# Where a block of expert results is parked between PSUM and memory: a buffer group of its own, eight deep

## The chip, the core and the metric

The kernel runs on one core of one Trainium2 chip. The metric is the device time of one execution in microseconds (us), and the figure given for a kernel is the median of its runs. The core has a matrix engine (PE, with its weight loads, PEld, beside it), a vector engine (DVE), a scalar engine (ACT), a general engine (POOL) and SyncE (SP), which here issues most DMAs. Each engine runs its own list of instructions in order, and one engine waits for another, or for a DMA to land, on a semaphore.

## The reference, cut to what matters

Thirty-two sequences of 56 tokens, each of width 256, with a context of 1500 rows each, go through two layers of a cross-attention and a feed-forward block of experts:

```python
x = x + _L0_xattn_ref(_layernorm(x), ctx_2048, ...)     # a decayed sum over the context, projected
x = x + _L0_ffn_ref(_layernorm(x), gate_w, w_gate, w_up, w_down)   # 16 experts of 176, 6 per token
x = x + _L1_xattn_ref(_layernorm(x), ctx_2048, mask)    # softmax attention over the context
x = x + _L1_ffn_ref(_layernorm(x), ...)                 # 2 experts of 1024, 1 per token
```

The change stands in the second of these. For each expert e the reference computes

```python
g = h @ w_gate[e].T
u = h @ w_up[e].T
out = jax.nn.silu(g) * u @ w_down[e].T
y = y + cw[:, e:e + 1] * out          # cw is zero outside a token's six experts
```

## The kernel before, in words

The program has four stages, one after the other: the context sums with the routing of tokens to experts (to about 210 us of the profile), the first experts (to about 513 us), the attention (to about 602 us) and the second experts (to the end).

In the first-experts stage the tokens have been sorted by expert into 99 blocks of 128 rows (`NB0`), padded where an expert's rows do not fill a block. `expert_blocks` (L769) runs over the blocks with a software pipeline written out by hand: in step t it issues the gate and up product of block t (`gate_up`, L778), turns the product of block t-1 (`turn`, L799), turns the input rows of block t+1 (`turned_rows`, L192), and issues the down product of block t-2 (`down`, L807). A step has twelve matmuls: four for `gu` (L785), two transposes of `hs` (L803), two transposes of the gathered rows (L195), and four for `y` (L812).

The order on every engine of this stage is the order of the Python code (`manual_schedule`, L928); no planner moves anything. Waits follow from the tile pools: a tile of a pool with n buffers waits until the tile n before it under the same tag has been used for the last time. The pools of the stage are `wk` (three buffers a tag: `sg`, `hs`, `hT`, `xT`, `yb`), `rt` (single tiles), `xbp` (eight buffers, used for the gathered rows `xb`), `resp` (six, for results `g` fetched back), and four PSUM pools of two banks each.

When a block's down product is finished, `done` (L949) copies it from PSUM to a tile `yb` on ACT (L951) and issues on SP a store of 128 KB to its place in `ys0` in device memory (L952). So `yb` of block n is written when the store of block n-3 has landed. On ACT the order of one step is: `sg` of block t (L791), `xT` of block t+1 (L197), `yb` of block t-2 (L951).

On SP each step has the store and, beside it, a part of other transfers that `side` (L1036) issues: windows of the context, 384 KB each (L174), in steps 1 to 16; the residual rows, 2 MB, in step 17 (L1050); a row of the mask (L1055) in steps 18 to 49, each with a register load of its start; and zeros, 771 KB each (L1067), five times between steps 18 and 30. On POOL each step has the gather of a block seven ahead (`rows_of`, L941), and in most steps a gather `result` (L853) of finished results from `ys0` for an early token group, which DVE adds to the residual (L1029).

After the stage the attention begins: SP loads sixteen further context windows into new buffers (`extra`, L174), and POOL gathers the remaining results from `ys0` with an adding DMA (`added`, L1317), which needs every store landed.

Of the kernel before, what the change touches and what calls it, by code (L numbers as in the profile page):

```python
# [8 lines left out]
F32 = mybir.dt.float32  # L9
# [10 lines left out]
P = 128  # L20
B, S, D, T = 32, 56, 256, 1500
# [37 lines left out]
def xattn_ffn_kernel(  # L59
# [174 lines left out]
    with tc.tile_pool(name="p1", bufs=1) as p1, tc.tile_pool(name="p3", bufs=3) as p3, tc.tile_pool(  # L234
        name="xn", bufs=4
    ) as xnp, tc.tile_pool(name="z", bufs=4) as zp, tc.tile_pool(name="p1_ps", bufs=5, space=PSUM) as ps, tc.tile_pool(
        name="p1_acc", bufs=2, space=PSUM
# [529 lines left out]
        V.tensor_copy(ei, ep[0:1, 0:P])  # L767

    def expert_blocks(nb, nq, f, w, ei, wk, ptr, pgu, pht, py, rows_of, done, ahead, wgt=None, side=None, xT0=None):  # L769

        fp = f // nq
# [35 lines left out]
        def down(i, u):  # L807
            if u == 0:
                y[i] = py.tile([P, 512], F32, tag="y", name="y")
            a = hT.pop((i, u))  # L810
            for c in range(2):
                PE.matmul(  # L812
                    y[i][:, 0:D], lhsT=a[:, c * P : (c + 1) * P],
                    rhs=w[0:h, bass.ds(at[i] + (u * piece + doff + c * D), D)],
                    start=(u == 0 and c == 0), stop=(u == nq - 1 and c == 1),
                )
            if u == nq - 1:
                done(i, y.pop(i))
# [109 lines left out]
    with tc.manual_schedule(  # L928
        engines={ET.PE, ET.DVE, ET.Activation, ET.SP, ET.Pool}
    ), tc.tile_pool(name="f0", bufs=3) as wk, tc.tile_pool(name="f0r", bufs=1) as rt, tc.tile_pool(  # L930
        name="f0x", bufs=8
    ) as xbp, tc.tile_pool(name="res0", bufs=6) as resp, tc.tile_pool(
        name="f0_tr", bufs=2, space=PSUM
    ) as ptr, tc.tile_pool(name="f0_gu", bufs=2, space=PSUM) as pgu, tc.tile_pool(
        name="f0_ht", bufs=2, space=PSUM
# [11 lines left out]
            return xb  # L947

        def done(i, y):  # L949
            yb = wk.tile([P, D], F32, tag="yb", name="yb")  # L950
            A.copy(yb, y[:, 0:D])  # L951
            nc.sync.dma_start(out=ys0[i * P : (i + 1) * P, :], in_=yb)  # L952

# [82 lines left out]
        def side(t):  # L1036
# [50 lines left out]
        expert_blocks(  # L1087
            NB0, 1, F0, w0_sb.rearrange("p e w -> p (e w)"), ei,
            wk, ptr, pgu, pht, py, rows_of, done, 7, wgt, side,
        )  # L1090
        assert not ways_ and not todo and not sums and not steps[NR]
# [20 lines left out]
    with tc.manual_schedule(  # L1112
        engines={ET.PE, ET.DVE, ET.Activation, ET.SP, ET.Pool}
    ), tc.tile_pool(name="at", bufs=2) as at, tc.tile_pool(name="ex", bufs=1) as ex, tc.tile_pool(name="at_x", bufs=4, space=PSUM) as px, tc.tile_pool(
        name="at_sc", bufs=1, space=PSUM
    ) as psc, tc.tile_pool(name="at_pt", bufs=2, space=PSUM) as ppt, tc.tile_pool(
        name="at_o", bufs=1, space=PSUM
# [271 lines left out]
    with tc.tile_pool(name="f1", bufs=3) as wk, tc.tile_pool(  # L1389
        name="f1_tr", bufs=2, space=PSUM  # L1390
    ) as ptr, tc.tile_pool(name="f1_gu", bufs=2, space=PSUM) as pgu, tc.tile_pool(
        name="f1_ht", bufs=2, space=PSUM
# [41 lines left out]
    with tc.If(nc.values_load(bad[0:1, 0:1], min_val=0, max_val=1)), tc.tile_pool(  # L1434
        name="g", bufs=2
    ) as gp, tc.tile_pool(name="g1", bufs=1) as g1, tc.tile_pool(
        name="g_tr", bufs=2, space=PSUM
    ) as ptr, tc.tile_pool(name="g_gu", bufs=2, space=PSUM) as pgu, tc.tile_pool(
        name="g_y", bufs=1, space=PSUM
# [175 lines left out]
```

## Time and profile before

| | |
|---|---|
| median of 3 runs | 755.1 us (752.46 to 756.65) |
| profiled execution, its own time | 789.92 us |
| span of its profile | 788.0 us |
| PE busy in the span | 680.0 us (86%) |
| ACT busy / DVE busy / POOL busy | 242.2 / 404.6 / 354.0 us |
| copies `yb` (L951) | 99, 375 ns each, 37.1 us |
| mean granted PE clock | 0.945 |

The profile is of one execution, and that one took 34.8 us longer than the median of the others. Busy shares are of the engine, not of its list of waits: an engine that waits on a semaphore is idle. Where an instruction waits for more than one semaphore, the compiler puts a separate wait (EVENT_SEMAPHORE) ahead of it, which the engine's own list runs in order too. Ends of matmuls are modelled in the profile. For waits, the profile names the instruction that came last by its own clock; where none fits it says "remote" or "unknown queue".

### The profile page before, as it was taken

The page shows a single profiled execution, that of the slowest core. Times are in us where ns is not written, and L with a number is a line of the kernel's source. Part 1 is how long each engine was busy: PE and PEld are TensorE (multiplying, and loading weights), DVE is VectorE, ACT ScalarE, POOL GpSimd, SP SyncE. Part 2 cuts the span into 40 slices and gives each one's busy share as a digit, 9 for nine tenths or more (in the row PEclk, how much of TensorE's full clock was granted, in tenths as well). Part 3 has the DMA queues.
Part 4 walks back from the last instruction along what each step waited for, and adds up shares of the span by engine and source line. Part 5 has one row for each costly group of instructions (what it writes and reads, how often), then busy time and mean ns, then how long its engine had stood idle before and what let it go on. Part 6 is the DMA issues. An engine that isn't in the chain of part 4 may idle for free.

```text
span 788.0 us, 13691 instructions
## 1 busy us (share of the span) xinstructions
PE 680.0 (86%) x4147; PEld 447.8 (57%) x4147; DVE 404.6 (51%) x1386; ACT 242.2 (31%) x716; POOL 354.0 (45%) x444
## 2 busy tenths in 40 slices
PE   3477988887789889889899889899797999999995
PEld 3334545554467667556667566666464566666663
DVE  3568677788436436234444345667587333233321
ACT  0123233333134333333333333366463111111110
POOL 5355566643343465556656665457542411122110
PEclk9879799997699999899999999999899999999998
DMA  8969899999258976334434444387961200110100
GB/s 260 351 258 376 321 346 381 359 340 238 72 161 269 329 224 197 107 106 137 133 114 131 133 133 134 107 251 181 257 224 48 94 13 21 41 35 27 33 27 18
DMA packets 71426, 137.69 MB, mean 175 GB/s; under 512 B 7859, under 2 KB 43844, under 8 KB 71348
## 3 DMA queue, kind: packets, MB, share of 16 engines
q1 hardware_dynamic: 56612, 100.84, 37.4%
q0 software_dynamic: 14736, 35.90, 16.9%
q8 instruction: 39, 0.64, 0.3%
q14 instruction: 39, 0.32, 0.1%
HBM read 110.07 MB, written 27.29 MB: 174 GB/s over the span
## 4 chain that ended last, share of the span: by engine, by line
PE 72%; DVE 7%; DMA 5%; ACT 3%; issue 3%; POOL 3%; another core or an unknown queue 1%; POOLq 0%; ACTq 0%; DVEq 0%
PE gu L785 29%; PE y L812 18%; PE acc L325 6%; PE tp L803 4%; PE tp L195 4%; DMA xr<-ys,back 4%; ACT xT L197 2%; PE owned L593 1%; POOL xr L1318 1%; PE bp L467 1%; PE lp L505 1%; POOL xn L491 1%; PE sT L459 1%; PE tp L913 1%
## 5 line engine op out<-in xcount | busy, mean ns | idle before, releaser
L785 PE MATMUL gu<-w_sb,xT 128*128 x396 | 142.1, 482 | 23.9 <-ACT xT L197 19.7
L943 POOL DMA_INDIRECT xb<-xn,idx x99 | 96.6, 976 | 103.1 <-PE tp L195 52.1
L791 ACT ACTIVATE sg<-gu 128x176 f32<-128x176 f32 (+1 forms) x159 | 54.4, 342 | 239.5 <-PE gu L785 206.9
L797 DVE SCALAR_TENSOR_TENSOR hs<-sg,wgt,gu 128x176 f32<-128x176 f32 x99 | 39.3, 397 | 158.4 <-ACT sg L791 136.3
L785 PE MATMUL gu<-ring,xT 128*128 x240 | 112.9, 593 | 0.5 <-issue 0.5
L785 PEld LDWEIGHTS gu<-w_sb,xT 128*128 128x128 f32 x396 | 73.6, 194 | 61.9 <-ACT xT L197 27.5
L812 PE MATMUL y<-w_sb,hT 88*128 x396 | 103.6, 384 | 0.8 <-ACT yb L951 0.8
L856 POOL DMA_INDIRECT g<-ys,early x78 | 74.0, 949 | 33.5 <-issue 18.0
L795 DVE TENSOR_TENSOR hs<-sg,gu 128x256 f32<-128x256 f32 x60 | 25.2, 421 | 112.5 <-ACT sg L791 110.2
L803 PEld LDWEIGHTS tp<-ident,hs 128*88 128x88 f32 (+1 forms) x318 | 41.3, 131 | 61.4 <-issue 48.4
L812 PEld LDWEIGHTS y<-w_sb,hT 88*128 88x128 f32 x396 | 68.6, 193 | 7.1 <-ACT yb L951 1.0
L1423 POOL DMA_INDIRECT out<-ob,ti x15 | 14.9, 990 | 127.4 <-DVE ob L1420 127.1
L805 DVE COPY hT<-tp 88x256 f32<-88x256 f32 (+1 forms) x159 | 66.0, 415 | 3.8 <-PE y L812 2.8
L197 ACT COPY xT<-tp 128x256 f32<-128x256 f32 x130 | 48.4, 372 | 56.9 <-PE tp L195 39.3
L785 PEld LDWEIGHTS gu<-ring,xT 128*128 128x128 f32 x240 | 45.3, 190 | 33.0 <-issue 30.1
L803 PE MATMUL tp<-ident,hs 128*88 128x128 f32 (+1 forms) x318 | 61.6, 276 | 0.7 <-DVE mv L871 0.6
L812 PE MATMUL y<-ring,hT 128*128 x240 | 61.7, 380 | 0.0
L951 ACT COPY yb<-y 128x256 f32<-128x256 f32 x99 | 37.1, 375 | 61.2 <-PE y L812 31.0
L325 PE MATMUL acc<-ring,cz 128*32 128x256 f32 x768 | 54.9, 444 | 0.3 <-DVE cz L301 0.3
L195 PE MATMUL tp<-ident,xb 128*128 128x128 f32 x228 | 44.8, 279 | 2.4 <-issue 2.4
L432 POOL TENSOR_SCALAR z<-xr,mva,rsa 128x256 f32<-128x256 f32 x16 | 23.0, 1437 | 49.6 <-DVE xr L479 45.4
L812 PEld LDWEIGHTS y<-ring,hT 128*128 128x128 f32 x240 | 41.0, 190 | 3.3
(306 smaller groups left out, 1000.8 us busy)
## 6 DMA issues: line engine op xcount, KB each, us to landing
ring<-in_cx SPq DMA_DIRECT2D x32, 1536.0 KB
ys<-yb SPq DMA_DIRECT2D x99, 128.0 KB
ring<-in_cx SPq DMA_DIRECT2D x16, 384.0 KB
extra<-in_cx SPq DMA_DIRECT2D x16, 384.0 KB
xs<-zrow SPq DMA_DIRECT2D x5, 771.0 KB
w_sb<-in_wg SPq DMA_DIRECT2D x2, 1408.0 KB
w_sb<-in_wu SPq DMA_DIRECT2D x2, 1408.0 KB
xn<-xn SPq DMA_DIRECT2D x16, 128.0 KB
```

The costliest lines, as they stand in the source:

```text
L195: PE.transpose(tp[:, k * P : (k + 1) * P], xn[:, k * P : (k + 1) * P], ident)
L197: A.copy(xT.rearrange("p k c -> p (k c)"), tp[:, 0 : KD * P])
L325: PE.matmul(acc[Q * g : Q * g + Q, 0:D], lhsT=cz[:, j, 1 - h : 1 - h + Q], rhs=c[:, j, :], start=(h == 0 and m == 0), stop=(h == 1 and m = ...
L785: PE.matmul(gu[:, 0 : 2 * fp], lhsT=xT[i][:, k, :], rhs=w[:, bass.ds(at[i] + (u * piece + k * 2 * fp), 2 * fp)], start=(k == 0), stop=(k = ...
L791: A.activation(sg, gu[:, 0:fp], AF.Silu)
L797: V.scalar_tensor_tensor(hs[i, u], sg, wgt[:, i : i + 1], up, ALU.mult, ALU.mult)
L803: PE.transpose(tp[0:h, c * P : (c + 1) * P], a[:, c * h : (c + 1) * h], ident)
L805: V.tensor_copy(hT[i, u], tp[0:h, 0 : 2 * P])
L812: PE.matmul(y[i][:, 0:D], lhsT=a[:, c * P : (c + 1) * P], rhs=w[0:h, bass.ds(at[i] + (u * piece + doff + c * D), D)], start=(u == 0 and c ...
L856: G.indirect_dma_start(out=g, out_offset=None, in_=ys0[0 : n * P, :], in_offset=bass.IndirectOffsetOnAxis(ap=at[:, p, k : k + 1], axis=0),)
L943: G.indirect_dma_start(out=xb, out_offset=None, in_=xn0, in_offset=bass.IndirectOffsetOnAxis(ap=idx[:, i : i + 1], axis=0),)
L951: A.copy(yb, y[:, 0:D])
```

## The change

One line of `done`: the tile `yb` is taken from the pool `xbp` with eight buffers of its own tag, in place of the pool `wk`, where it had three. `xbp` keeps its eight buffers for `xb`; the tag `yb` has eight more beside them.

```diff
         def done(i, y):
-            yb = wk.tile([P, D], F32, tag="yb", name="yb")
+            yb = xbp.tile([P, D], F32, tag="yb", bufs=8, name="yb")
             A.copy(yb, y[:, 0:D])
             nc.sync.dma_start(out=ys0[i * P : (i + 1) * P, :], in_=yb)
```

No instruction is added, removed or moved on any engine. A buffer is 1 KB in each partition, so the stage holds 5 KB a partition more, and tiles that were allocated after `yb` lie at other addresses; a few of the waits that come from reusing the memory of the stage before, or that pass it on to the stage after, differ for that reason.

## The prediction

> **What bounds the kernel now.** I read the page first, for the span and the chain that ended last, then the stage's busy times by stretches, then who waited for whom between 226 and 513 us, and last the instructions of single steps.
>
> ```profile
> span 788.0 us, 13691 instructions
> ...
> PE 72%; DVE 7%; DMA 5%; ACT 3%; issue 3%; POOL 3%; another core or an unknown queue 1%; POOLq 0%; ACTq 0%; DVEq 0%
> ...
> L812 PE MATMUL y<-w_sb,hT 88*128 x396 | 103.6, 384 | 0.8 <-ACT yb L951 0.8
> ...
> L951 ACT COPY yb<-y 128x256 f32<-128x256 f32 x99 | 37.1, 375 | 61.2 <-PE y L812 31.0
> ```
>
> The chain is PE's. The copy `yb` has 61.2 us of idle ACT time ahead of it, but most of it ends with PE finishing `y`: that is ACT having nothing to do, not a full ring of buffers. The stretches of the stage:
>
> ```profile
> core 0: us, PE busy (x) PEld busy (x) DVE busy (x) ACT busy (x) POOL busy (x), PEclk, DMA share, GB/s
> 230.00:265.00 35.00, 35.00 (x170) 26.25 (x169) 21.73 (x73) 14.89 (x43) 13.35 (x15) 1.00 0.89 273
> 265.00:320.00 55.00, 46.95 (x218) 33.47 (x218) 24.12 (x95) 19.34 (x56) 32.62 (x34) 0.99 0.73 236
> 320.00:400.00 80.00, 71.24 (x317) 50.84 (x317) 27.98 (x82) 27.08 (x79) 47.97 (x50) 0.95 0.42 121
> 400.00:500.00 100.00, 89.72 (x420) 64.51 (x419) 44.58 (x136) 35.08 (x104) 58.58 (x62) 0.98 0.44 126
> ```
>
> In the first stretch PE is busy all the time, although the DMA engines are 0.89 busy: steps of 2.49 us (the copies stand at 232.63 and 235.12 us), back to back. Later PE loses 10 to 15% of its time. The question is whether full `yb` buffers cost any of that. The waits of ACT and PE in the stage:
>
> ```profile
> ACT yb L951 <- PE y L812: 31.0, 47, 3.4
> ...
> ACT yb L951 <- remote: 4.4, 2, 2.3
> ...
> PE gu L785 <- ACT xT L197: 18.2, 17, 2.2
> PE tp L902 <- ACT yb L951: 5.4, 2, 2.8
> ```
>
> No wait of `yb` is put down to a store. Only the two "remote" ones (before the copies at 318.53 and 340.36 us) could be, and behind them PE waited 5.4 us. Each copy after the third has its wait as a separate instruction:
>
> ```profile
> L951 ACTq EVENT_SEMAPHORE  x96: 38/791/3703, 231.8 to 511.5; - x96
> ```
>
> It holds two semaphores, the store three blocks back and PE's count. I compared each end with the semaphore updates that the trace records. Twenty of the 96 last under 60 ns: all was there. In 57 an update of PE comes within 60 ns before the end. In the other 19 no update is recorded so close, but that of the store is 5.6 us old or more. None ends with its store. The two "remote" ones: the store's last update is at 311.73 us and PE's at 318.463, the wait ends at 318.489; and 333.03, 340.296, 340.323. The longest (3.70 us, to 375.18) ends 26 ns after five PE updates begin to come in a burst. So what ran late there is PE's count, by up to 3 us behind its modelled end.
>
> Second reading, by the DMA packets: counted off in order of issue, a store lands 1.33 to 6.42 us after its issue, median 2.09. The store that a copy needs had landed 0.76 us (block 19) to 11.9 us before its product was ready, median 5.6.
>
> **What the Trainium skill says.** "Perfetto Trace Analysis", section "Optimization Strategy", says that a gap which repeats on the engine that should be saturated can mean too few buffers for the next tile. The gaps of this stage do not fit: they come now and then, and where traffic is heaviest (230 to 265 us) there are none. The same page, "DMA Instruction — HWDGE", warns that the last descriptor, which updates the semaphore, can be long delayed when the target is HBM; here that is in the 1.33 to 6.42 us. Its section "Identifying Dependency Chains" says that an instruction that waits on several engines may get separate semaphore waits ahead of it, which is the row above.
>
> **The change part by part.** All engines keep their instructions and order.
>
> (1) The wait for store n-3 becomes one for store n-8. Removed: 0 us on this profile, since no wait ended with it. What would a late store cost? Here is one step:
>
> ```profile
> 232.63 0.37 ACT L951 COPY yb<-y 128x256 f32<-128x256 f32 x1 [0.48 <-PE y L812]
> 233.03 0.57 SPq L952 DMA_DIRECT2D ys<-yb  x1
> 233.77 0.32 ACT L791 ACTIVATE sg<-gu 128x176 f32<-128x176 f32 x1 [0.77 <-PE gu L785]
> 234.26 0.37 ACT L197 COPY xT<-tp 128x256 f32<-128x256 f32 x1 [0.17 <-PE tp L195]
> 234.87 1.35 PE L785 MATMUL gu<-w_sb,xT 128*128 x4
> ```
>
> Behind `yb` on ACT stand `sg` and `xT`; PE waits for `xT`. ACT is idle 0.77 us before `sg`, and after `xT` (ends 234.63) PE has 0.24 us left; `sg` and `xT` can follow closer, 0.21 us apart as at 354.37 and 354.58 in another step. So `sg` may start 0.47 us late (234.24 + 0.21 + 0.37 + 0.05 = 234.87), `yb` 0.77 + 0.47 = 1.24 us. The store has 3 x 2.49 = 7.47 us less copy and issue (0.45) = 7.0 us, and 8.2 us before PE feels it. The longest measured, from the end of copy 17 (268.02) to its landing (275.41, SP issued it only at 269.98), is 7.4.
>
> (2) The ACT wait loses one condition (a wait for ACT's own earlier copy, met long before), and the wait on PE moves from the separate instruction to the copy. `yb` begins 0.08 us after PE's modelled end, `sg`, whose wait on PE is its own, 0.04: at most 0.04 us x 99 = 4 us of ACT, in the 0.77 us of idle ACT time ahead of `sg`. On the path 0; if that cover were gone, 4 us.
>
> (3) SP. The stores now name a lane of their own that the old ACT wait had covered: the store about four blocks back, since stores and other DMAs alternate over eight lanes. That one lands before store n-3. 0 us. Behind it on SP stand windows and mask rows needed tens of us later.
>
> (4) Moved addresses. `zrow`'s memset on POOL waits for more of the stage before, the latest being DVE's one-hot tile (L571, ends 203.41 us instead of a start at 200.21). Then 0.53 + 0.10 us, done by 204.1; the next on POOL, the first gather, starts at 209.53 for its indices. Cover 5.4 us, cost 0. The first `yb` and the first mask row get waits for transfers of the first stage, met long before; the first store loses such waits.
>
> (5) Handover to attention. The first `extra` load waited for all eight lanes, the last store among them (wait over at 515.10, issue 515.19); now its own wait list has one lane, PE, DVE and POOL. SP reached it at 514.65, so it goes about 0.4 us earlier. No one waits there for windows. The chain instead is the last store's landing, then POOL's adding gathers, of which four stand in it with 7.70, 7.84, 6.98 and 8.65 us; the loads compete with the first three. I put this at 0, with ±0.4 us for the shift.
>
> Sum: 0 + 0 + 0 + 0 ± 0.4 on 789.92 us of the profiled execution, so 790. That one stands 34.8 us above the median. The late PE counts make up such a sum: copies start 40.2 us later, over all 99, than 0.08 us after their product's modelled end. If the other runs have fewer of these, steps come closer to 2.49 us and stores have less time. At that pace block 20 would be ready at 270.06 + 2 x 2.49 = 275.04 and store 17 lands at 275.41: 0.4 us late, under the 1.24 us that costs nothing. So the median too stays: 755 us.
>
> **The rivals.**
>
> *Stores do fill three buffers in the unprofiled runs (faster).* Steps then take (L + 0.45)/3, L from copy to landing. For: store 17 needed 7.4 us, and 2 MB, 771 KB five times and the gathers fall between 265 and 305 us. Against: every other store there is shorter, and PE never waited for one. At L = 8.6 us over the 13 or so blocks of that stretch: (9.05/3 - 2.49) x 13 = 6.8 us, so 748. It decides from L over 8.2.
>
> *The attention's start is hindered (slower).* The extra loads go out before the last store has landed; the four adding gathers in the chain sum to 31.2 us. If each becomes 1.4 us longer, the time is 755 + 5.6 = 761. For: they share DMA engines that are 0.84 to 1.09 busy from 515 to 535 us. Against: the loads wait in SP's queue behind that store, and shift by 0.4 us only. It decides from 12% longer gathers (3.8 of 31.2 us).
>
> *The change doesn't do what it says:* SP, by its lanes, still holds stores to about four blocks in flight, so eight buffers are never in use. Likely true and without cost: ACT only needs its own buffer. Time 755.
>
> **How the numbers follow.** Same, 0.76 (the forecast and the third rival, which end alike); faster 0.15; slower 0.09. About 0.5%, 3.8 us, is what a measurement of this kernel can tell from no change: its three runs spread over 4.2 us. The likeliest case spans 752 to 758; to leave out no more than two in ten I take half of the faster case's reach and some of the slower one's: 750 to 759. What pulls the range open is (2) without cover, 4 us, and the unprofiled pace.
>
> **What would show it.** After: no `yb` wait ended by a store, as before; steps of 2.49 us from 230 to 265 us; PE busy in the stage within a few us of before; the first `extra` issue at once after the last store's. Wrong if the stage is over 4 us shorter with PE's waits for `xT` gone, or the adding gathers longer than 8 us each.

## The result, and the profile after

The changed kernel takes 750.5 us (median of 16 runs, 745.95 to 753.94) against 754.5 us of the kernel before (16 runs, 752.04 to 756.65): a ratio of 0.9948, 95% interval [0.9932, 0.9963]. It is faster by 4.0 us, just over the 0.5% that the prediction took as its bound. The range of 750 to 759 us holds it, by 0.5 us; the likeliest case, "the same" at 752 to 758 us, does not.

The profile on which the prediction rests is of an execution of 789.92 us, and later sets of runs came out whole either at about 753 us (called ordinary below) or at 790 to 797 us (called long), for both kernels alike and once on the same chip, so kernels are compared within one set, and the traces of before that are shown below are of a repeat of the unchanged kernel (753.28 us, span 751.3 us).

The page of the changed kernel, with the lines that answer to those shown of before (span; the chain that ended last, by engine; then two groups, with busy us and mean ns, and after the second bar the idle time ahead of them):

```profile
span 748.1 us, 13687 instructions
...
PE 78%; DVE 8%; ACT 3%; DMA 2%; POOL 2%; issue 2%; POOLq 0%; DVEq 0%; ACTq 0%
...
L812 PE MATMUL y<-w_sb,hT 88*128 x396 | 102.0, 380 | 0.0
...
L951 ACT COPY yb<-y 128x256 f32<-128x256 f32 x99 | 36.8, 372 | 44.5 <-PE y L812 44.1
```

The chain is PE's still. Busy times by stretches, first of the changed kernel, then one stretch of the repeat of the kernel before:

```profile
core 0: us, PE busy (x) PEld busy (x) DVE busy (x) ACT busy (x) POOL busy (x), PEclk, DMA share, GB/s
230.00:265.00 35.00, 35.00 (x170) 26.42 (x169) 21.27 (x70) 14.86 (x42) 13.17 (x14) 1.00 0.88 267
265.00:320.00 55.00, 53.54 (x260) 40.22 (x259) 26.88 (x107) 23.48 (x66) 36.81 (x39) 1.00 0.78 250
320.00:400.00 80.00, 78.69 (x391) 59.56 (x390) 37.70 (x105) 34.83 (x97) 56.06 (x61) 1.00 0.51 148
400.00:500.00 100.00, 97.95 (x539) 70.27 (x540) 56.15 (x176) 47.78 (x131) 64.42 (x65) 1.00 0.64 183
```

```profile
265.00:320.00 55.00, 52.83 (x253) 39.05 (x252) 26.14 (x103) 22.90 (x65) 36.69 (x40) 1.00 0.74 240
320.00:400.00 80.00, 78.66 (x391) 59.45 (x390) 37.19 (x104) 34.53 (x98) 56.80 (x60) 1.00 0.50 146
```

In the profiled execution of the prediction PE was busy 46.95 of 55 us and 71.24 of 80 us in these stretches. In an execution of ordinary length it is 52.83 and 78.66 us with three buffers as well: the 10 to 15% of idle PE time that the prediction set out to explain belongs to the long executions, not to the kernel. With eight buffers the first of the two has 0.71 us more, the second the same.

Now the waits. First of the repeat of before from 226 to 480 us (who waited for whom: us in total, times, longest), then the separate wait instruction ahead of each copy (ns, shortest/median/longest):

```profile
ACT yb L951 <- PE y L812: 45.5, 94, 0.9
...
ACT yb L951 <- DMA ys<-yb: 3.7, 2, 2.8
...
PE gu L785 <- ACT xT L197: 0.8, 1, 0.8
```

```profile
L951 ACTq EVENT_SEMAPHORE  x96: 38/791/1216, 229.1 to 473.0; - x96
```

And of the changed kernel:

```profile
ACT yb L951 <- PE y L812: 43.7, 97, 0.9
...
ACT yb L951 <- DMA ys<-yb: 0.4, 1, 0.4
```

```profile
L951 ACTq EVENT_SEMAPHORE  x93: 17/17/38, 223.5 to 473.4; - x93
```

With three buffers two copies, those of blocks 19 and 20, do wait for a store, up to 2.8 us, and PE then waits for `xT`. With eight, PE's wait for `xT` is gone. The one entry of 0.4 us that is left is no wait for a store: 0.44 us is the idle time ahead of an ordinary copy that waits for PE. The separate wait has shrunk to 17 ns, since the wait on PE now sits on the copy itself.

The place, in the repeat of before on ACT (start, us, instruction, in brackets the idle time before it and what ended it):

```profile
269.11 0.37 ACT L197 COPY xT<-tp 128x256 f32<-128x256 f32 x1 [0.17 <-PE tp L195]
270.38 0.37 ACT L951 COPY yb<-y 128x256 f32<-128x256 f32 x1 [0.90 <-DMA ys<-yb]
...
271.59 0.37 ACT L197 COPY xT<-tp 128x256 f32<-128x256 f32 x1 [0.17 <-PE tp L195]
274.77 0.37 ACT L951 COPY yb<-y 128x256 f32<-128x256 f32 x1 [2.81 <-DMA ys<-yb]
275.04 0.32 ACT L791 ACTIVATE sg<-gu 128x176 f32<-128x176 f32 x1
275.25 0.38 ACT L197 COPY xT<-tp 128x256 f32<-128x256 f32 x1
```

and behind it on PE:

```profile
275.68 1.45 PE L785 MATMUL gu<-w_sb,xT 128*128 x4 [0.83 <-ACT xT L197]
```

The copy of block 20 has its product at 272.37 us and starts at 274.77, when store 17 has landed (274.67). `sg` and `xT` follow at once, 0.21 us apart, and PE's next `gu` is late. The landings here are read from the store's semaphore. The Trainium skill, "DMA: Bandwidth & Descriptors", section "Why a DMA increments its semaphore by 16 and not by 1", says that only the full 16 means that all data has landed. In this trace the fifteenth increment of store 17 is at 273.59 us and the sixteenth at 274.67, 0.10 us before the copy starts. From the end of their copies, stores 16 to 19 take 7.60, 9.31, 7.71 and 5.46 us here; all others 4.96 us or less.

The same copy in the changed kernel:

```profile
274.02 0.37 ACT L951 COPY yb<-y 128x256 f32<-128x256 f32 x1 [0.44 <-PE y L812]
```

It starts 0.04 us after its product, and 2.33 us before its store 17 has landed (276.35): this store is as late as before, and nothing waits for it.

Why these four are late shows on SP (start and duration of DMA issues):

```profile
260.58 0.43 SPq L1050 DMA_DIRECT2D xr<-xr  x1
262.70 1.84 SPq L952 DMA_DIRECT2D ys<-yb  x1
265.99 0.33 SPq L1055 DMA_DIRECT2D wrow<-in_mask  x1
266.42 0.94 SPq L1067 DMA_DIRECT2D xs<-zrow  x1
267.45 0.60 SPq L952 DMA_DIRECT2D ys<-yb  x1
```

Store 16 (262.70) follows the 2 MB of residual rows (L1050) and its issue alone takes 1.84 us, where the store before takes 0.32. Store 17, whose copy ended at 265.36, is issued at 267.45, behind a mask row and 771 KB of zeros.

To compare executions I use two readings of each trace. One is the time from the copy of block 15 to that of block 33 (18 steps, 44.78 us at 2.49 us each). The other is the number of copies that start over 0.5 us later than 0.08 us after their product's modelled end. In the traces of ordinary length:

| kernel | copy 15 to copy 33 | late copies, lateness in all | PE steps over 2.49 us there |
|---|---|---|---|
| before, repeated (three buffers) | 46.07 us | 2, 3.0 us | +0.20, +1.09 us |
| after (eight) | 44.78 us | 0 | none |

The stretch holds 1.29 us of the difference, 1.09 of it behind copy 20 (the 0.20 stands at block 17, before any late copy). That is less than the 4.0 us of the medians, and the experiments are about both: whether the store is the cause, and what the rest is.

### The profile page after: what moved, and what is told of

Same layout as the page of the kernel before. It is cut to its first block, busy times and chain, and to the rows that moved or that the text cites. A ratio compares the mean times of both kernels' runs of the same rounds, so it can differ in the third digit from the quotient of the medians.

```text
span 748.1 us, 13687 instructions
## 1 busy us (share of the span) xinstructions
PE 666.1 (89%) x4147; PEld 446.2 (60%) x4147; DVE 403.8 (54%) x1386; ACT 245.9 (33%) x716; POOL 352.4 (47%) x444
## 4 chain that ended last, share of the span: by engine, by line
PE 78%; DVE 8%; ACT 3%; DMA 2%; POOL 2%; issue 2%; POOLq 0%; DVEq 0%; ACTq 0%
PE gu L785 29%; PE y L812 18%; PE acc L325 7%; PE tp L803 4%; PE tp L195 4%; PE tp L913 2%; PE sp L1139 2%; PE op L1174 2%; PE owned L593 2%; PE bp L467 1%; PE lp L505 1%; DMA xr<-ys,back 1%; POOL xn L491 1%; PE sT L459 1%; DVE st L183 1%
## 5 line engine op out<-in xcount | busy, mean ns | idle before, releaser
L785 PE MATMUL gu<-w_sb,xT 128*128 x396 | 136.6, 467 | 3.6 <-ACT xT L197 2.1
L943 POOL DMA_INDIRECT xb<-xn,idx x99 | 94.4, 954 | 64.6 <-PE tp L195 44.0
L812 PE MATMUL y<-w_sb,hT 88*128 x396 | 102.0, 380 | 0.0
L325 PEld LDWEIGHTS acc<-ring,cz 128*32 128x32 f32 x768 | 28.2, 127 | 25.5 <-issue 13.7
```

The source lines that it names most:

```text
L325: PE.matmul(acc[Q * g : Q * g + Q, 0:D], lhsT=cz[:, j, 1 - h : 1 - h + Q], rhs=c[:, j, :], start=(h == 0 and m == 0), stop=(h == 1 and m = ...
L785: PE.matmul(gu[:, 0 : 2 * fp], lhsT=xT[i][:, k, :], rhs=w[:, bass.ds(at[i] + (u * piece + k * 2 * fp), 2 * fp)], start=(k == 0), stop=(k = ...
L812: PE.matmul(y[i][:, 0:D], lhsT=a[:, c * P : (c + 1) * P], rhs=w[0:h, bass.ds(at[i] + (u * piece + doff + c * D), D)], start=(u == 0 and c ...
L943: G.indirect_dma_start(out=xb, out_offset=None, in_=xn0, in_offset=bass.IndirectOffsetOnAxis(ap=idx[:, i : i + 1], axis=0),)
```

## The experiments

Theory A: with three buffers the stores behind the 2 MB transfer are late by some us, two copies wait, and PE loses about 1.3 us; nothing else changes. Theory B: the move between pools, with its changed waits at the stage's ends, makes the gain. Theory C came later: deep buffers also gain on PE's granted clock.

### The kernel before, once more

No edit.

> The kernel before, unchanged, to see an execution that is not 35 us above the median. Both theories: ratio 1.000 (0.998 to 1.002). Theory A (stores three blocks back are late where the 2 MB and the zeros are in flight): the profile shows some copies yb between 265 and 290 us whose wait ends with a store, and PE idle for 1 to 4 us in all behind them. Theory B (the gain is in the handover to attention, where the first extra load no longer waits for the last store): all steps of the first experts are as in the changed kernel, and the attention stage, from the last yb copy to the first gu of the second experts, is longer than its 87.4 us by about 4 us.

Measured: 753.71 us, ratio 1.0008 [0.9989, 1.0026]. The trace is the one shown above. Its time from the end of copy 98 to the first product of the second experts is 88.26 us, against 87.43 after: not the 4 us that B needs there.

### The pool alone, the depth alone, and four buffers

```diff
-            yb = wk.tile([P, D], F32, tag="yb", name="yb")
+            yb = xbp.tile([P, D], F32, tag="yb", bufs=3, name="yb")   # the pool alone
+            yb = wk.tile([P, D], F32, tag="yb", bufs=8, name="yb")    # the depth alone
+            yb = xbp.tile([P, D], F32, tag="yb", bufs=4, name="yb")   # four buffers
```

> Three buffers as before, but in the pool xbp, so that the addresses and the wait lists at both ends of the stage are nearly those of the changed kernel; the depth is not. Theory A: as before, ratio 1.000, with the late stores of before in 265 to 290 us. Theory B: as the changed kernel, ratio 0.995.

> Eight buffers, but left in the pool wk, so that the first extra load still waits for the last stores as before. Theory A: as the changed kernel, ratio 0.995. Theory B: as before, ratio 1.000.

> Four buffers in the pool xbp. Theory A: a store then has 4 x 2.49 - 0.45 = 9.5 us instead of 7.0, and the longest in the changed kernel's profile took 8.0 us from copy to landing, so it is as the changed kernel, ratio 0.995, or at least three quarters of the way. Theory B: also 0.995, so this one only tells how deep the ring must be if A holds.

| kernel | us | ratio to before | copy 15 to copy 33 | late copies, in all |
|---|---|---|---|---|
| other pool, three buffers | 753.38 | 1.0001 [0.9987, 1.0015] | 46.36 us | 3, 5.4 us |
| old pool, eight buffers | 752.78 | 0.9986 [0.9963, 1.0008] | 44.78 us | 0 |
| other pool, four buffers | 750.96 | 0.9972 [0.9955, 0.9990] | 44.78 us | 0 |

B falls: the pool alone gives nothing and has the late copies as before; the depth alone removes them in the old pool. That is read from the traces: the time of the old pool with eight buffers is not clear of no change by itself, and neither reaches the 0.995 that was expected. Four buffers are enough: in the trace with eight the longest store takes 9.42 us from its copy (8.0 in the expectation), less than four steps of 2.49 us. The waits of ACT and PE with three buffers in the other pool:

```profile
ACT yb L951 <- DMA ys<-yb: 5.1, 3, 3.3
...
PE gu L785 <- ACT xT L197: 1.3, 1, 1.3
```

### The changed kernel again, and three others, in a long set

```diff
# one kernel: three buffers, the 2 MB store left out
-            if t == B // 2 + 1:
-                nc.sync.dma_start(
-                    out=xr0.rearrange("(p r) d -> r p d", r=P), in_=xr,
-                )
# another: three buffers, the 2 MB cut into sixteen pieces of 128 KB
+            if B // 2 + 1 <= t < B // 2 + 1 + NP:
+                q = t - B // 2 - 1
+                nc.sync.dma_start(out=xr0[q * P : (q + 1) * P, :], in_=xr[:, q, :])
# a third: two buffers
-            yb = xbp.tile([P, D], F32, tag="yb", bufs=8, name="yb")
+            yb = xbp.tile([P, D], F32, tag="yb", bufs=2, name="yb")
```

> The changed kernel once more, unaltered. Theory A (only late stores count): the stretch from the copy of block 15 to that of block 33 takes 44.8 us against 46.1 with three buffers, and the rest of the first comparison's 4 us was the granted clock falling differently in the two sets of runs; then the ratio to the kernel before is 0.9975 to 0.9985, with the clock's share alike. Rival C (deep buffers also gain on the clock, each time): the ratio is again 0.995, with about 1.5 us less lost to the clock than in the runs of the kernel before beside it.

> The kernel before with three buffers, but without the 2 MB store of the residual rows in step 17 (this part of the work is left out; it is only read back in a branch that is not taken). Theory A1 (this transfer is what makes stores 16 to 19 late): no copy of blocks 18 to 24 waits for a store, the stretch from copy 15 to copy 33 takes 44.8 us, and the time is 1.3 us shorter, ratio 0.998. Rival A2 (the zeros, 771 KB each, and SP's own queue make them late): a store still takes over 8.2 us from copy to landing in that stretch, it takes 45.8 us or more, and the ratio is 1.000.

> The kernel before with three buffers and all of its work, but the 2 MB store of the residual rows cut into sixteen of 128 KB, one in each of steps 17 to 32. Theory A1 (the burst in front of stores 16 to 19 is the cause): the stores of that stretch land within 7 us of their copy, the stretch from copy 15 to copy 33 takes 44.8 to 45.2 us, ratio 0.998 with the old three buffers. Rival A2 (SP's queue and the zeros): with one more issue on SP in each step it gets worse, stores land later than 8.2 us, the stretch takes over 46 us, ratio 1.000 to 1.004.

> The changed kernel with two buffers instead of eight. Theory A: a store then has 2 x 2.49 - 0.45 = 4.5 us, and PE feels it from 5.8 us. Stores 16 to 20 take 7.6, 9.3, 7.7, 5.5 us with three buffers; block 19 would wait for store 17 about 5.3 us, 4 us of it on PE, later ones less, since every wait also gives the stores behind it time: the stretch from copy 15 to copy 33 takes 48.5 to 50 us and the whole 2.5 to 4 us more than before, ratio 1.003 to 1.005. The rest of the stage stays, as its stores land within 4.5 us. Rival (depth counts for little, the difference was in the clock): stretch under 47 us, ratio 1.000.

In this set the kernel before took 796.62 us (59 runs, 790.25 to 806.48), and all four lay on it:

| kernel | us | ratio to before | copy 15 to copy 33 | late copies, in all |
|---|---|---|---|---|
| after, repeated | 796.39 | 1.0017 [0.9988, 1.0045] | 52.00 us | 29, 43.0 us |
| three buffers, no 2 MB store | 797.47 | 0.9989 [0.9960, 1.0019] | 52.25 us | 26, 45.4 us |
| three buffers, 2 MB in pieces | 797.07 | 0.9990 [0.9965, 1.0015] | 52.43 us | 28, 41.8 us |
| two buffers | 796.89 | 0.9989 [0.9963, 1.0014] | 52.56 us | 24, 46.4 us |

The ratios of 1.000 would be the rivals', but the set tells the theories apart no more than it does the kernels: all of them need PE's steps of 2.49 us, which are not there from 265 us on. The changed kernel itself has 29 late copies with eight buffers, which a full ring of three can't explain. Its stretches and waits:

```profile
265.00:320.00 55.00, 49.10 (x233) 35.85 (x232) 25.81 (x101) 19.82 (x59) 31.40 (x33) 1.00 0.75 245
320.00:400.00 80.00, 67.86 (x310) 48.14 (x309) 29.35 (x87) 27.60 (x80) 49.77 (x52) 0.98 0.42 124
```

```profile
PE gu L785 <- ACT xT L197: 22.0, 19, 3.3
...
ACT yb L951 <- remote: 6.3, 2, 5.2
```

These look like the profile that the prediction used (18.2 us of PE's waits for `xT`, "remote" waits of `yb`, 28 late copies with 38.2 us in all). So that profile was of such a time, and there the depth gives no gain that can be measured: the changed kernel is at 1.0017 [0.9988, 1.0045].

The one without the 2 MB store and the one with two buffers were run again, on another chip:

> Three buffers, without the 2 MB store of the residual rows in step 17 (that part of the work is left out), for a chip on which the kernel before takes 753 us. On a chip where it takes 796 us, PE's counts come late in bursts whatever the depth, and no depth or traffic changed the time; if this is such a chip again, all theories expect 1.000 here. Otherwise, theory A1 (this transfer makes stores 16 to 19 late): no copy of blocks 18 to 24 waits for a store, the stretch from copy 15 to copy 33 takes 44.8 us against 46.1, ratio 0.998. Rival A2 (the zeros, 771 KB each, and SP's own queue make them late): a store still takes over 8.2 us from copy to landing there, the stretch 45.8 us or more, ratio 1.000.

> Two buffers instead of eight, for a chip on which the kernel before takes 753 us (on one where it takes 796 us, 1.000 again). Theory A: a store has 4.5 us, and PE feels it from 5.8 us; block 19 waits for store 17 about 5.3 us, 4 us of it on PE, later ones less: the stretch from copy 15 to copy 33 takes 48.5 to 50 us, the whole 2.5 to 4 us more than before, ratio 1.003 to 1.005, and outside the stretch nothing changes. Rival (depth counts for little, the first comparison's difference was in the clock): stretch under 47 us, ratio 1.000.

The kernel before took 792.37 us there (43 runs), without the store 792.45 us, ratio 1.0004 [0.9979, 1.0028], with two buffers 789.88 us, 0.9967 [0.9941, 0.9993]; the stretch 52.56 and 53.97 us, 23 and 25 late copies with 39.2 and 41.6 us. The first is as expected of such a set. The second lies just below 1, where 0.9989 in the first long set did not; with two readings I don't take it as shown that fewer buffers help there.

### The cause and the dose, in an ordinary set

The same two kernels a third time. The chip was that of the first long set; now the kernel before took 752.91 us on it (31 runs, 750.23 to 756.43).

> Three buffers, without the 2 MB store of the residual rows in step 17 (that part of the work is left out), a third time. Where the kernel before takes about 753 us: theory A1 (this transfer makes stores 16 to 19 late) expects no copy of blocks 18 to 24 over 0.5 us after its product, the stretch from copy 15 to copy 33 at 44.8 us, ratio 0.998; rival A2 (zeros and SP's own queue) expects two or three such copies with 3 to 5.4 us in all, the stretch at 45.8 us or more, ratio 1.000. Where it takes 790 us or more: 1.000 by either, with some 25 copies over 0.5 us late, 40 us in all, as in each such profile so far.

> Two buffers, a third time. Where the kernel before takes about 753 us: theory A expects copy 19 about 5.3 us late and the stretch from copy 15 to copy 33 at 48.5 to 50 us, ratio 1.003 to 1.005; the rival (depth counts for little) under 47 us and 1.000. Where it takes 790 us or more: theory A by itself 1.000; if holding the copies back lessens what delays PE's counts there (the last such run gave 0.9967), again 0.996 to 0.998.

| kernel | us | ratio to before | copy 15 to copy 33 | late copies, in all |
|---|---|---|---|---|
| three buffers, no 2 MB store | 751.98 | 0.9982 [0.9968, 0.9995] | 44.97 us | 0 |
| two buffers | 756.41 | 1.0058 [1.0032, 1.0084] | 48.76 us | 3, 8.6 us |

The first is as theory A1 had it. Without the transfer no copy waits, with the old three buffers; the stretch has only the 0.20 us at block 17 left. The same zeros and mask rows were issued, so rival A2 falls: without the 2 MB ahead of them no store in the stretch takes over 5.5 us (5.50, block 26). How much the zeros add when the 2 MB are there was not measured. Two buffers on ACT:

```profile
271.82 0.37 ACT L951 COPY yb<-y 128x256 f32<-128x256 f32 x1 [4.08 <-DMA ys<-yb]
...
275.10 0.37 ACT L951 COPY yb<-y 128x256 f32<-128x256 f32 x1 [2.42 <-DMA ys<-yb]
```

Copy 18 starts when store 16 lands (271.72), copy 19 when store 17 does (275.00), 3.54 and 4.33 us late (5.3 was expected of the second; the first had already held the pipeline up). From product to product PE's steps are 3.82 and 0.17 us longer, which is the stretch's 48.76 - 44.78 = 3.98 us. Not all of it is the wait. PE's clock was granted at half from 273.80 to 277.21 us, in the middle of this place; the other ordinary traces have no such window in the stretch. By the 1.24 us of slack that the prediction worked out, a lateness of 4.33 us would cost PE 3.09 us by itself; the other 0.9 us is left to the slower clock. So the wait alone would give 44.78 + 3.09 = 47.9 us, between what theory A (48.5 to 50) and its rival (under 47) expected: theory A has the direction and the copies, and had the size too large. Whether PE's wait brought the half clock with it, one trace can't show.

The time agrees. The ratio, 1.0058, is a little more than the 2.7 us of the stretch against three buffers (1.0036), which its interval still holds. With the clock's part taken off each run (as under "The size" below), two buffers take 1.8 ± 0.5 us more than three, and the waits alone account for 3.09 - 1.09 = 2.0 us.

## Why the prediction was right or wrong

**The range.** It holds 750.5 us, in part by luck. The forecast was no change. The low end was drawn down to 750 for the rival that was given 0.15, and that rival's mechanism is the one that happened. Its shown size, 1.1 to 1.6 us, would have left the median inside the likeliest case, where "the same" would have looked right with the mechanism wrong; 2.4 to 2.9 us that no store explains brought it to the edge of the range.

**What bounds the kernel.** Right that PE's chain does, and that late PE counts fill the idle time of the profile. But that is true of the long executions alone. In an ordinary one the gaps of the stage are small, and between copies 15 and 33 the full buffers make the largest. The prediction saw the 34.8 us between its profile and the median, and drew the right inference ("steps come closer to 2.49 us and stores have less time"); it then sized that case with landings measured in the other.

**(1), the removed wait at 0 us: this is the step that failed.** Its tolerance was exact. It put the lateness of a copy that costs PE nothing at 1.24 us; the traces give 2.33 us late and 1.09 us lost (repeat of before), 2.82 us late and 1.58 us lost (other pool, three buffers), and both differ by 1.24; copy 19 of the repeat, 0.42 us late, costs nothing. Its allowance of 7.0 us from copy to landing, 8.2 before PE feels it, holds too. The term that was mis-sized is the landing of store 17: put at 7.4 us, "0.4 us late, under the 1.24 us that costs nothing", it takes 9.31 and 9.81 us in ordinary executions with three buffers. There are two reasons. The packets, counted off over all engines, give a time that is too early: in the repeat of before the count gives about 272.8 us and the semaphore's sixteenth increment 274.67. So the delay of the last update, which the prediction took to lie within its 1.33 to 6.42 us, was outside them here. And in the trace that the prediction had, store 17 has two of its sixteen increments recorded, the later at 275.86 us: later than the 275.41 that was used, and itself a lower bound only. A lower bound was used as a value, for the one store that decides.

**"None ends with its store"** is false of the kernel: 2 of 96 waits in the repeat do, 3 with three buffers in the other pool. It is not certain of the profile read either, since "under 60 ns: all was there" does not follow. In the repeat the separate waits ahead of copies 19 and 20 are recorded with 38 ns each, though ACT stood idle 0.90 and 2.81 us and both ended with a store: the recorded length leaves out the time in which the store was waited for. In the profile read, one of the twenty short waits, ahead of copy 20, has 0.58 us of idle ACT time before it, and most increments of its store 17 are missing. Nothing hung on it there: the copy is 0.10 us late.

**(2) to (4), at 0 us.** Held. The separate wait on ACT shrank as described and `yb` starts 0.04 us after the product in place of 0.08. The memset of `zrow` moved to 204.08 us (from 198.90 in the repeat of before), done at 204.76, still 5 us ahead of the first gather. The pool alone, at three buffers and with most of the moved waits of (3) and (4), gave 1.0001 [0.9987, 1.0015]. The wait of (2) is not moved in it; in the three kernels with four or eight buffers it is, and the steps between copies 15 and 33 are 2.49 us there.

**(5), the handover, at 0 with ±0.4 us.** Held: the first of the context loads is issued 2.06 us after the last `yb` copy starts, in place of 2.54, so 0.5 us earlier, and nothing follows from it. The slower rival, longer adding gathers, didn't come: of the adding gathers' issues on POOL the first stands at 477.65 us and the eighteenth at 516.50 after, 477.30 and 516.16 before.

**The rivals.** "Stores do fill three buffers (faster)" had the mechanism and the threshold for a single late store (over 8.2 us), and was put at 748 us because it took 8.6 us for 13 blocks. It is one store over the threshold by 1.1 to 1.6 us, so the time lost is that, once. (Had 13 stores in a row been late, the prediction's own formula, (L + 0.45)/3 against 2.49, gives a loss from 7.0 us on, not 8.2, since the slack is there only once.) "The change doesn't do what it says" was half right: with at most four blocks copied and not yet landed in the trace of the changed kernel, buffers five to eight are never needed, but the fourth is, which the prediction denied.

**The size.** The shown mechanism gives 1.1 to 1.6 us, a ratio of 0.998 to 0.9985. The kernels with the wait removed lie at 0.9986, 0.9972 and 0.9982, whose intervals hold that. The first comparison's 0.9948 [0.9932, 0.9963] doesn't: 2.4 to 2.9 us of its 4.0 are not explained by the store. Part of it may be the clock. In the two traces shown the spans differ by 3.2 us. Of that 1.29 us lie between copies 15 and 33; 2.75 us lie in the second experts, where the kernels are the same and 5.60 us of clock were lost before against 2.77 after; the stretch up to the first copy goes the other way, 1.81 us longer after with 3.42 us more lost.

Over all runs, span times the share of clock not granted (the most that the clock can have cost, since some of it falls where PE is idle) is 37.25 ± 0.76 us (mean and its error over the runs) for the changed kernel, and 38.77 ± 0.31 and 37.92 ± 0.43 us for the kernel before in the two other ordinary sets; without it the changed kernel stands at 713.2 ± 0.4 and before at 714.6 ± 0.2 and 715.0 ± 0.3, a difference of 1.5 to 1.8 us, near the mechanism's. The other kernels order themselves in the same way: 713.6 with four buffers, 713.9 with eight in the old pool, 715.0 and 715.3 with three in the other pool and in the repeat of before, 716.8 with two. For the runs of before in the first comparison no clock is on record. Whether deep buffers gain on the clock each time (theory C) stays open: eight buffers in the old pool lost as much to it as before (38.66 ± 0.86 us), four in the other less (37.43 ± 0.61), and the repeat of the changed kernel, which would have told, fell into a long set. So a change whose shown effect lies within 0.5% was measured just outside it, and I can't say which part of the excess would come again.

## What to carry to other kernels

A ring of n buffers is too short when one transfer out of it outlasts n steps by more than the slack of the engines that wait behind it; look for that at the store behind the largest burst, and read the landing from the last increment of its semaphore, in an execution whose time is that of the median. If the profiled execution is far from the median, ask first what a normal one would look like, and treat durations from it as bounds. Here one buffer more was enough, and so was the burst's absence; cutting it into pieces was not measured at ordinary pace.

## What the runs showed of the hardware

- The same program takes about 753 us or 790 to 797 us, by the set of runs. One chip gave 796.62 us of the kernel before in one set and 752.91 in a later one; another gave 792.37. The extra time is in the first-experts stage: in the two traces of the changed kernel 38 of 46 us lie between copies 15 and 98 (251.4 against 213.3 us, 3.4 us of it lost to the clock). In each of seven long traces 23 to 29 copies start over 0.5 us late by PE's modelled ends, 38 to 46 us in all; in the ordinary ones 0 to 3. What holds PE's counts back is open; eight buffers, the 2 MB transfer left out and its division made no difference to the time there that is clear of noise, and two buffers gave 0.9989 and 0.9967.
- The clock comes and goes in steps. A stage of a trace often loses 1.71, 3.41 or 6.83 us to it, or nothing. The Trainium skill, "TensorE: Matmul & The Clock Gate", section "Part 1: The HAM clock gate (the "warmup" mystery)", has half rate in windows of about 3.4 us, whose place is not tied to the kernel's start; one, two or four such windows at half rate are these losses, so the traces agree. Effects of 1 to 3 us are of that size, and the medians carry it.
- A store of 128 KB usually lands 1.7 to 5 us after its copy. Behind 2 MB it took up to 9.8, of which 2.2 us is SP not having issued it yet (2.0 to 2.4 us for store 17 in the six ordinary traces that have the 2 MB). Without the 2 MB it was issued 0.02 us after its copy and landed 4.4 us after it.
- A separate wait on two semaphores is recorded with 38 ns although the engine stood idle for up to 2.81 us before it (copy 20 of the repeat of before), so its length doesn't tell how long was waited.
